# Query and key products of each half of the tokens as seven block products on shared sums, with the tokens split by quarters

## The chip, the cores and the metric

The program runs on one core of a Trainium2 chip. The core has TensorE (PE in the profile; PEld is its loading of weights), VectorE (DVE), ScalarE (ACT), GpSimd (POOL) and SyncE (SP, which here only issues DMAs). They run side by side, each in its own fixed order, and wait for one another through semaphores. The metric is the time of one execution on the device in microseconds (us), lower is better: 2119.15 us is the median of three runs before the change (2118.79 to 2119.32).

## The reference

x has 8 batches of 1024 tokens of 512 values (float32). Cut to what matters:

```python
xn = _layernorm(x)                      # LN(x)
q = xn @ Wq                             # 512 -> 128
gate = softmax(xn @ Wg)                 # 3 gates a token
for i in range(3):
    k = xn @ Wk[i]                      # 512 -> 128
    v = xn @ Wv[i]                      # 512 -> 128
    w = decay[i] ** max(s - t - 1, 0) * (s > t)
    blended += gate[..., i:i+1] * ((q @ k.T) * w) @ v
s = blended @ Wo * out_scale
h = silu(xn @ lut[gate_idx].T) * (xn @ lut[up_idx].T)     # 1376 wide
g = silu(h @ lut[down_idx].T)
out = x + s * g
```

The weights of the feed-forward are indices into a table of 16 values. q and the three k together are one product of LN(x), 512 values, with a matrix of 512 columns.

## The kernel before

The kernel has two phases. Phase 1 computes LN(x), the attention part, and the looked-up feed-forward weights, and leaves its results in DRAM. Phase 2 computes the feed-forward and the output.

**Phase 1** runs over batches b. For a batch, `project` (L361) loads x in 8 chunks of 128 tokens, last chunk first, normalises each chunk, transposes it on PE into `xnT` (pt, L411, copied by ACT at L412), and computes pv (L418), which holds v and the logits of the gates; ACT copies it out (L421). In pv the slice of `xnT` just copied is the stationary operand, which PE loads as weights. `features(hf, j)` (L448) computes for a half hf of 512 tokens q^T (j=0) or one k_i^T (j=1 to 3) as four matmuls 128x512 into one PSUM bank pq (L455), which ACT copies to `qT` or `kT` (L458). Half 1 is done while chunks 3 to 0 are projected, one j a chunk; half 0 in the first four chunk steps of the next batch.

At the same time `chunks` (L523) works on the batch before: a decayed state runs over its chunks from the last to the first. In a chunk step PE does pk (transposes of k, L552), psc (k times gated q, L561), pu (the state's update, L569), and po (L583) in two groups, first state times qb, then v times pr. Between them DVE does ga (L536, gates times q^T; the gates come from DRAM, broadcast to all partitions) and pr (L563, psc times the decays), POOL qb (L540), and ACT ks (L555), R (L588), the scaling of pu (L595) and bl (L584). The gates go through DRAM: they are written transposed (gTd, L442) and read back as ga (L446).

The step of a chunk is written out by hand: the main loop at L637 to L662 advances the generators of the older batch, the newer batch, what is left of the batch before it (`ending`), and the build of the feed-forward weights in a fixed interleaving. `keep_order` then holds the order of PE, DVE, ACT and POOL as traced; SP's order is the scheduler's. `defer` and `tick` put a DMA a few parts later. I number the steps of a batch k=0 to 7: in k=0 to 3 half 0 of the batch before gets its features, in k=4 to 7 half 1 of the batch being projected.

PSUM has 8 banks in phase 1: `p_a` with 4, shared by pt, pv and pq, `p_c` with 3, shared by pk, psc and po, and one for pu.

**Sums of LN(x)^T.** The feed-forward multiplies 2x2 blocks with seven products in place of eight, on two levels. For the outer level it needs four sums t1 to t4 of the blocks of LN(x)^T; the blocks b11, b12, b21, b22 are the two halves of the 512 values by the two halves of the tokens. DVE forms them at L512, one 128x1024 operation in each of the steps k=0 to 3, and SP writes xnT and the sums to `xs_d` (L519 to L521).

**Weights** (`ffn_weights`, L246). DVE looks up 128 rows of gate and up weights (L217 to L241), POOL forms the sums of the inner level (L270 to L274) and, for a pair of such blocks, the outer sums in `pair` (L289 to L295); the lower block's own second quarter is written by a DMA of its own (L287) and the pair's four parts by another (L296).

**Phase 2** works on PE in groups of seven products (L783, four matmuls 128x256 each), then the down projection (L1037) and the output with Wo (L1152).

Of the kernel before, what the change touches and what calls it, by code (L numbers as in the profile page):

```python
# [48 lines left out]
def recurrent_block(ctx: ExitStack, tc, x, wq, wk, wv, wo, wg, decay_logits, out_scale, lut, gidx, uidx, didx, out):  # L49
# [25 lines left out]
    U = 512  # L75
    NC = T // P
# [89 lines left out]
    def tables():  # L166

        nc.sync.dma_start(out=dl, in_=decay_logits.partition_broadcast(P))
        nc.sync.dma_start(out=lut_sb, in_=lut.partition_broadcast(P))
        nc.sync.dma_start(out=osc, in_=out_scale.partition_broadcast(P))
        nc.gpsimd.iota(e_int, pattern=[[0, NI]], base=0, channel_multiplier=1)
        nc.gpsimd.memset(e_c, float(P))
        nc.gpsimd.memset(zero, 0.0)
        nc.sync.dma_start(out=pow_d[:, :P], in_=zero)
        yield

        nc.vector.tensor_scalar(dl, dl, -87.0, None, ALU.max)  # L180
        nc.scalar.activation(dec, dl, AF.Exp, scale=-1.0)
        nc.vector.tensor_copy(e_k, e_int)
        nc.vector.tensor_tensor(lut_x, lut_i[:, :, 0:1], lut_i[:, :, 1:2], ALU.bitwise_xor)
        yield
        nc.vector.tensor_scalar(dec, dec, 1.0, None, ALU.add)
        nc.vector.reciprocal(dec, dec)
        nc.gpsimd.tensor_tensor(k_tab, dec, e_k, ALU.pow)
        nc.gpsimd.tensor_tensor(c_tab, dec, e_c, ALU.pow)

        def write():  # L190
            with nc.allow_non_contiguous_dma(reason="384 words, once"):
                nc.sync.dma_start(out=pow_d[:, P:].rearrange("i s -> s i"), in_=k_tab)

        defer(4, write)
        for _ in range(4):
            yield
        backs = []
        for step, first in ((1, 0), (0, P)):
            back = small.tile([P, NI, P], F32, name="back", tag="back", bufs=2)
            nc.sync.dma_start(  # L200
                out=back, in_=bass.AP(pow_d.tensor, pow_d.offset + first, [[step, P], [2 * P, NI], [1, P]])
            )
            backs.append(back)
        yield
        for tab, back in zip((w_tab, q_tab), backs):
            nc.vector.tensor_copy(tab, back[:, :, ::-1])
            yield
# [38 lines left out]
    def ffn_weights(build, pool, pair_pool):  # L246
# [6 lines left out]

        upper = []

        def gate_up(o):
# [28 lines left out]
            pair = pair_pool.tile([P, 7, 4, P], F32, name="pair", tag="pair")  # L285
            nc.sync.dma_start(out=to[:, :, 0:2, :], in_=up)
            defer(3, lambda: nc.sync.dma_start(out=to[:, :, 2, :], in_=low[:, :, 1, :]))  # L287
# [5 lines left out]
            nc.gpsimd.tensor_tensor(pair[:, :, 2], b11, b21, ALU.subtract)  # L293
            yield
            nc.gpsimd.tensor_tensor(pair[:, :, 3], b12, pair[:, :, 1], ALU.subtract)  # L295
            defer(4, lambda: nc.sync.dma_start(out=to[:, :, 3:7, :], in_=pair))  # L296
# [12 lines left out]
        def down(rows, e, ends):  # L309
# [21 lines left out]
            pair = pair_pool.tile([P, 7, 4, P], F32, name="pair", tag="pair")  # L331
# [10 lines left out]
            defer(4, lambda: nc.sync.dma_start(out=to[:, :, 4:7, :], in_=pair[:, :, 0:3]))  # L342
# [12 lines left out]
    def warm_up(n):  # L355

        warm = p_a.tile([P, P], F32, name="warm", tag="a")
        for _ in range(n):
            nc.tensor.matmul(warm, lhsT=ident, rhs=ident, start=True, stop=True)

    def project(b, pools, sides, kept):  # L361
# [6 lines left out]
        wvg_sb, wqk_sb = sides  # L368
# [4 lines left out]
        qT, kT = {}, {}  # L373
        gates = []
        kept[b] = (v_sb, gates, qT, kT)
# [32 lines left out]
        def transpose(c):  # L408
            pt = p_a.tile([P, NV, P], F32, name=f"pt{b}_{c}", tag="a")
            for v in range(NV):  # L410
                nc.tensor.transpose(pt[:, v, :], xts[c][:, ts(v, P)], ident)  # L411
            nc.scalar.copy(xnT[:, :, ts(c, P)], pt)  # L412

        def values(c):

            pv = p_a.tile([P, NI * D + NI], F32, name=f"pv{b}_{c}", tag="a")
# [31 lines left out]
        def features(hf, j):  # L448

            if j == 0:  # L450
                qT[hf] = att.tile([P, U], F32, name=f"qT{b}_{hf}", tag=f"qT{hf}", bufs=1)
                kT[hf] = att.tile([P, NI, U], F32, name=f"kT{b}_{hf}", tag=f"kT{hf}", bufs=1)
            pq = p_a.tile([P, U], F32, name=f"pq{b}_{hf}_{j}", tag="a")
            for v in range(NV):
                nc.tensor.matmul(  # L455
                    pq, lhsT=wqk_sb[:, v, ts(j, D)], rhs=xnT[:, v, ts(hf, U)], start=(v == 0), stop=(v == NV - 1)
                )
            nc.scalar.copy(qT[hf] if j == 0 else kT[hf][:, j - 1, :], pq)  # L458
# [23 lines left out]
        for k in range(NC):  # L482
# [11 lines left out]
            if k >= NC // 2:  # L494
                if lag and k == NC // 2:
                    values(c + 1)
                    lag = 0
                features(1, k - NC // 2)
# [4 lines left out]
            if k >= lag:  # L503
                values(c + lag)
            yield
        ts_ = tp.tile([P, 4, 2, U], F32, name=f"ts{b}", tag="ts")
        b11, b12, b21, b22 = (xnT[:, 2 * r : 2 * r + 2, ts(hf, U)] for r in (0, 1) for hf in (0, 1))
        t1, t2, t3, t4 = (ts_[:, k] for k in range(4))
        sums = ((t1, b12, b11), (t2, b22, t1), (t3, b22, b12), (t4, b21, t2))
        for k in range(NC // 2):  # L510
            yield
            nc.vector.tensor_tensor(*sums[k], ALU.subtract)  # L512
            features(0, k)
# [3 lines left out]
            next(half, None)  # L517
            yield
        nc.sync.dma_start(out=xs_d[b][:, 0:4, :], in_=xnT[:, :, :U])  # L519
        nc.sync.dma_start(out=xs_d[b][:, 4:6, :], in_=b22)  # L520
        defer(2, lambda: nc.sync.dma_start(out=xs_d[b][:, 6:14, :], in_=ts_.rearrange("p a b u -> p (a b) u")))  # L521

    def chunks(b, pools, kept):  # L523

        chk, blp = pools
        v_sb, gates, qT, kT = kept.pop(b)
# [5 lines left out]
        def gated(c):  # L532
# [3 lines left out]
            nc.vector.tensor_tensor(qa, qa, qT[hf][:, ts(k, P)].unsqueeze(1).to_broadcast([P, NI, P]), ALU.mult)  # L536
# [7 lines left out]
        for c in reversed(range(NC)):  # L544
# [3 lines left out]
            kc = kT[c // (NC // NHALF)][:, :, ts(c % (NC // NHALF), P)]  # L548
# [51 lines left out]
    def phase_1():  # L600
        nonlocal small, p_a, p_c, p_r
        with (
            tc.tile_pool(name="p_a", bufs=4, space=PSUM) as p_a,
# [17 lines left out]
            wqk_sb = wts.tile([P, NV, (NI + 1) * D], F32, name="wqk_sb", tag="wqk_sb")  # L621

# [4 lines left out]
            warm_up(12)  # L627
            kept = {}
            ending = iter(())
            newer = project(0, pools, (wvg_sb, wqk_sb), kept)  # L630
            setup = tables()
# [5 lines left out]
            for b in range(B + 1):  # L637
                following = project(b + 1, pools, (wvg_sb, wqk_sb), kept) if b + 1 < B else iter(())
                older = chunks(b - 1, (chk, blp), kept) if b else iter(())
                for k in range(NC):  # L640
# [22 lines left out]
                    if (b, k) == (0, 3):  # L663
                        keep_order(tc, seen, (mybir.EngineType.SP,))
# [14 lines left out]
    H = U // 2  # L679
    ORDER = (1, 6, 5, 7, 2, 3, 4)  # L680

    def phase_2():
        with (
# [76 lines left out]
            class Node:  # L760
# [20 lines left out]
                def product(self, n, i, start=False):  # L781
                    for a in range(2):
                        nc.tensor.matmul(  # L783
                            self.t[n][:, ts(a, H)],
                            lhsT=self.w[:, a, (0, 1, 6, 2, 3, 4, 5)[i - 1], :],
# [301 lines left out]
            def down(b, h, h_tail, bl, ahead, beside):  # L1087
# [11 lines left out]
                def load(half, pool, tag):  # L1099
                    xr[half] = pool.tile([P, 4, V], F32, name=f"gx{b}_{half}", tag=tag)  # L1100
                    for n in range(4):
                        hold(out=xr[half][:, n], in_=x[b, ts(4 * half + n, P), :])
# [47 lines left out]
                def result(k):  # L1150
                    ps = next_bank(f"ps{b}_{k}")
                    nc.tensor.matmul(ps, lhsT=bl[:, ts(k, P)], rhs=wo_sb, start=True, stop=True)  # L1152
# [4 lines left out]
                    (nc.sync if b == B - 1 else nc.gpsimd).dma_start(out=out[b, ts(k, P), :], in_=o)  # L1157
# [176 lines left out]
```

## Time and profile before

| | |
|---|---|
| median of three runs | 2119.15 us (2118.79 to 2119.32) |
| the profiled execution, its own time | 2119.36 us |
| its span | 2117.6 us |
| phase 1, from 0 to the first matmul fs (L731) of phase 2 | 603.93 us |
| phase 2 | 1513.67 us |
| one chunk step of phase 1, pk to pk, with a batch being projected (k=0 to 6) | 9.48 us |
| PE busy, 0 to 603.93 us | 601.89 us |
| DVE busy, 0 to 603.93 us | 476.51 us |
| ACT busy, 0 to 603.93 us | 359.89 us |
| POOL busy, 0 to 603.93 us | 280.43 us |
| granted clock of PE in both phases | 1.00 |

The page's lines give, for a group of instructions, the line of the program, the engine, the operation, the output and input tiles, partitions by elements, and the count; then busy time in us, the mean of one in ns, and the idle time before them with what ended it. A timeline line begins with the start in us from the span's start and the duration. A float32 matmul of the program is two PE instructions, so four matmuls are x8. The starts of successive PE lines give the time that a group takes; its printed duration includes a tail that the next group overlaps.

### The profile page before, as it was taken

The page shows a single profiled execution, that of the slowest core. Times are in us where ns is not written, and L with a number is a line of the kernel's source. Part 1 is how long each engine was busy: PE and PEld are TensorE (multiplying, and loading weights), DVE is VectorE, ACT ScalarE, POOL GpSimd, SP SyncE. Part 2 cuts the span into 40 slices and gives each one's busy share as a digit, 9 for nine tenths or more (in the row PEclk, how much of TensorE's full clock was granted, in tenths as well). Part 3 has the DMA queues.
Part 4 walks back from the last instruction along what each step waited for, and adds up shares of the span by engine and source line. Part 5 has one row for each costly group of instructions (what it writes and reads, how often), then busy time and mean ns, then how long its engine had stood idle before and what let it go on. Part 6 is the DMA issues. An engine that isn't in the chain of part 4 may idle for free.

```text
span 2117.6 us, 31134 instructions
## 1 busy us (share of the span) xinstructions
PE 2109.2 (100%) x11306; PEld 1678.6 (79%) x11306; DVE 1409.2 (67%) x2150; ACT 929.4 (44%) x2083; POOL 1021.2 (48%) x1046
## 2 busy tenths in 40 slices
PE   9999999999999999999999999999999999999999
PEld 6666666666678888887879888887978888797877
DVE  6889888678545774576567556656755665675557
ACT  3666666666434414423441442344145324423531
POOL 2554565253354537416642752655275255527432
PEclk9999999999999999999999999999999999999999
DMA  7556557565464644464455446444544634464442
GB/s 195 158 176 160 190 174 169 181 129 177 110 252 153 240 168 153 156 236 140 146 195 185 151 148 245 139 147 172 208 151 154 246 123 155 165 218 148 152 154 109
DMA packets 164271, 361.45 MB, mean 171 GB/s; under 512 B 52083, under 2 KB 90230, under 8 KB 163094
## 3 DMA queue, kind: packets, MB, share of 16 engines
q1 hardware_dynamic: 149702, 336.12, 48.7%
q0 software_dynamic: 4480, 14.68, 1.7%
q10 hardware_dynamic: 9936, 8.66, 1.4%
q8 instruction: 90, 1.47, 0.3%
q14 instruction: 63, 0.52, 0.1%
HBM read 282.87 MB, written 76.55 MB: 170 GB/s over the span
## 4 chain that ended last, share of the span: by engine, by line
PE 98%; DVE 1%; DMA 1%; POOL 0%; issue 0%; ACTq 0%; ACT 0%; SPq 0%; POOLq 0%; DVEq 0%
PE s L783 33%; PE pq L455 10%; PE pv L418 8%; PE sE L783 6%; PE s12d L1037 5%; PE s21d L1037 5%; PE s11d L1037 5%; PE po L583 4%; PE fs L731 3%; PE pd L1145 3%; PE ps L1152 3%; PE sEd L1037 2%; PE psc L561 2%; PE pu L569 2%; PE pt L411 1%; PE fsE L731 1%
## 5 line engine op out<-in xcount | busy, mean ns | idle before, releaser
L783 PE MATMUL s<-xs,wq 128*128 128x256 f32 x3264 | 731.2, 379 | 0.0
L783 PEld LDWEIGHTS s<-xs,wq 128*128 128x128 f32 x3264 | 619.6, 190 | 95.8 <-issue 8.1
L806 DVE TENSOR_TENSOR s<-s,e 128x512 f32<-128x512 f32 x136 | 95.1, 699 | 204.1 <-ACT s L805 204.0
L455 PE MATMUL pq<-xnT,wqk_sb 128*128 128x512 f32 x512 | 230.3, 592 | 0.0
L1116 POOL TENSOR_TENSOR cu<-cu 128x256 f32<-128x256 f32 x32 | 34.8, 1088 | 306.7 <-DVE cl L1115 306.7
L418 PE MATMUL pv<-wvg_sb,xnT 128*128 128x387 f32 x512 | 177.6, 489 | 0.3 <-DMA wvg_sb<-in_wv 0.3
L714 POOL TENSOR_TENSOR xs<-xs 128x256 f32<-128x256 f32 x224 | 170.8, 789 | 4.5
L455 PEld LDWEIGHTS pq<-xnT,wqk_sb 128*128 128x128 f32 x512 | 92.4, 190 | 92.1 <-issue 91.8
L810 DVE TENSOR_TENSOR sE<-s,e 128x512 f32<-128x512 f32 x136 | 95.0, 699 | 104.9 <-PE s L783 104.9
L874 POOL TENSOR_TENSOR u<-u,e 128x512 f32<-128x512 f32 x64 | 79.9, 1270 | 148.7 <-DVE u L870 130.2
L801 ACT COPY e<-sE 128x512 f32<-128x512 f32 x136 | 79.6, 585 | 138.8 <-PE sE L783 138.5
L783 PE MATMUL sE<-xs,wq 128*128 128x256 f32 x544 | 139.6, 379 | 0.0
L397 POOL TENSOR_SCALAR rstd<-rstd 128x1 f32<-128x1 f32 x56 | 27.8, 497 | 229.6 <-ACT junk L396 229.0
L418 PEld LDWEIGHTS pv<-wvg_sb,xnT 128*128 128x128 f32 x512 | 92.7, 190 | 54.8 <-issue 2.4
L878 POOL TENSOR_TENSOR h<-h,u 128x512 f32<-128x512 f32 x64 | 80.1, 1272 | 113.1 <-DVE u L885 103.5
L794 ACT COPY s<-s 128x512 f32<-128x512 f32 x136 | 77.5, 570 | 109.2 <-PE s L783 105.1
L805 ACT COPY s<-s 128x512 f32<-128x512 f32 x136 | 77.5, 570 | 97.6 <-PE s L783 97.6
L1037 PE MATMUL s12d<-wdd,z 128*128 128x128 f32 x896 | 118.5, 275 | 0.6 <-ACT s12d L1059 0.6
L783 PEld LDWEIGHTS sE<-xs,wq 128*128 128x128 f32 x544 | 103.4, 190 | 14.0
L1037 PEld LDWEIGHTS s12d<-wdd,z 128*128 128x128 f32 x896 | 109.1, 192 | 0.8 <-ACT s12d L1059 0.8
L224 DVE TENSOR_SCALAR leaf<-idx,lut_x,lut_sb 128x1024 int32<-128x1024 int32 (+2 forms) x119 | 101.3, 876 | 0.0
L563 DVE TENSOR_TENSOR pr<-psc,w_tab 128x384 f32<-128x384 f32 x64 | 35.5, 555 | 92.0 <-PE psc L561 91.8
(236 smaller groups left out, 4254.3 us busy)
## 6 DMA issues: line engine op xcount, KB each, us to landing
wq<-quadd SPq DMA_DIRECT2D x112, 896.0 KB, 4.5
wdd<-wdd SPq DMA_DIRECT2D x56, 896.0 KB, 4.8
xs<-xsd SPq DMA_DIRECT2D x56, 512.0 KB, 6.6
wq<-quadd SPq DMA_DIRECT2D x48, 448.0 KB, 4.1
x<-in_x SPq DMA_DIRECT2D x64, 256.0 KB, 5.9
xsd<-ts SPq DMA_DIRECT2D x8, 2048.0 KB, 7.5
gx<-in_x SPq DMA_DIRECT2D x64, 256.0 KB, 5.4
out<-gx POOLq DMA_DIRECT2D x56, 256.0 KB, 2.3
```

What stands on the lines that cost most here:

```text
L224: nc.vector.tensor_scalar(o.bitcast(I32), iv, lut_x[:rows, k, :], lut_i[:rows, k, 0:1], ALU.bitwise_and, ALU.bitwise_xor,)
L418: nc.tensor.matmul(pv, lhsT=xnT[:, v, ts(c, P)], rhs=wvg_sb[:, v, :], start=(v == 0), stop=(v == NV - 1))
L455: nc.tensor.matmul(pq, lhsT=wqk_sb[:, v, ts(j, D)], rhs=xnT[:, v, ts(hf, U)], start=(v == 0), stop=(v == NV - 1))
L583: nc.tensor.matmul(po, lhsT=lh, rhs=rh, start=(n == 0), stop=(n == len(prods) - 1))
L714: nc.gpsimd.tensor_tensor(o, x1, x2, ALU.subtract)
L731: nc.tensor.matmul(ps, lhsT=w[:, 2 * W_OF[k] + n, :m], rhs=xs[:, X_OF[k], 2 * n : 2 * n + 2, :], start=start and n == 0, stop=stop and n == 1,
L783: nc.tensor.matmul(self.t[n][:, ts(a, H)], lhsT=self.w[:, a, (0, 1, 6, 2, 3, 4, 5)[i - 1], :], rhs=self.xs[:, X_OF[self.ks[a]], D_OF[i], : ...
L806: nc.vector.tensor_tensor(self.t[1], self.t[1], self.e, ALU.add)
L810: nc.vector.tensor_tensor(self.t[3], self.t[2], self.e, ALU.add)
L874: nc.gpsimd.tensor_tensor(o[:, n], o[:, n], other[:, n], ALU.add)
L878: nc.gpsimd.tensor_tensor(of_h(half, n), of_h(half, n), two(other[:, n]), ALU.mult)
L1037: nc.tensor.matmul(self.t[n][:, ts(a, P)], lhsT=self.lhs[i][:, e, ts(a, P)], rhs=self.w[:, e, D_OF[i], :], start=start and a == 0 and e == ...
```

## The change

q^T and the three k_i^T of a half are now one 2x2 block product of seven products. The blocks of the weights are [512 values in two halves] by [q and k_0, k_1 and k_2]; the blocks of LN(x)^T are the two halves of the 512 values by two quarters of 256 tokens. POOL forms the four sums of the weights once (`sums_of_weights`), after step k=3 of batch 0. DVE forms the sums t1 to t4 of LN(x)^T for each half, in steps k=4 and 5 (half 1) and k=0 and 1 (half 0); the same sums go to DRAM for the feed-forward, so its outer split of the tokens is now even and odd quarters instead of halves, and the last part of phase 2 takes its rows of x, bl and the output in that order (`place`).

A product is four matmuls 128x256. The seven lie in four steps, in this order: 1 and 5, 6 and 2, 7 and 3, then 4. In k=0 to 3 the second of a step stands on PE between psc and pv; in k=4 to 7 it stands behind pv. Partial results run on in PSUM: ACT copies bank pa to pb and pb to pc, later products add to them, and there are 6 ACT copies and 2 DVE additions a half in place of 4 ACT copies.

The four banks of `p_a` are now pa, pb, pe and pc; pt and pv move to the three banks of `p_c`. `write_banks` gives two of the banks their first write from PE, by 8 of the 12 matmuls with which PE was warmed up. The `pair` tile of the weights has three parts instead of four, one sum is formed in the place of b21, and two DMAs become one; for the block rows from 8 on POOL's third sum comes four parts later.

```diff
-        def features(hf, j):
...
-            pq = p_a.tile([P, U], F32, name=f"pq{b}_{hf}_{j}", tag="a")
-            for v in range(NV):
-                nc.tensor.matmul(
-                    pq, lhsT=wqk_sb[:, v, ts(j, D)], rhs=xnT[:, v, ts(hf, U)], start=(v == 0), stop=(v == NV - 1)
-                )
-            nc.scalar.copy(qT[hf] if j == 0 else kT[hf][:, j - 1, :], pq)
+        def features(hf):
+            qk[hf] = att.tile([P, NI + 1, U], F32, name=f"qk{b}_{hf}", tag=f"qk{hf}", bufs=1)
+            c11, c12, c21, c22 = (qk[hf][:, 2 * j : 2 * j + 2, ts(c, H)] for j in (0, 1) for c in (0, 1))
+            ts_ = tp.tile([P, 4, 2, H], F32, name=f"ts{b}_{hf}", tag=f"ts{hf}")
+            b11, b12, b21, b22 = (xnT[:, 2 * v : 2 * v + 2, ts(2 * hf + c, H)] for v in (0, 1) for c in (0, 1))
+            t1, t2, t3, t4 = (ts_[:, k] for k in range(4))
+            a11, a12, s3, a22 = (wqk_sb[:, 2 * v : 2 * v + 2, ts(j, 2 * D)] for j in (0, 1) for v in (0, 1))
+            s1, s2, s4 = (wqs[:, k] for k in range(3))
+            lhs = {1: a11, 2: a12, 3: s4, 4: a22, 5: s1, 6: s2, 7: s3}
+            rhs = {1: b11, 2: b21, 3: b22, 4: t4, 5: t1, 6: t2, 7: t3}
+            pa, pb, pe, pc = (p_a.tile([P, 2, H], F32, name=f"{r}{b}_{hf}", tag=r) for r in ("pa", "pb", "pe", "pc"))
+            def product(ps, k, start=False):
+                for j in range(2):
+                    for v in range(2):
+                        nc.tensor.matmul(
+                            ps[:, j, :],
+                            lhsT=lhs[k][:, v, ts(j, D)],
+                            rhs=rhs[k][:, v, :],
...
+            there = xs_d[b][:, :, ts(hf, H)]
+            nc.vector.tensor_tensor(t1, b12, b11, ALU.subtract)
+            yield
+            product(pa, 1, True)
+            nc.scalar.copy(pb, pa)
+            nc.vector.tensor_tensor(t2, b22, t1, ALU.subtract)
+            nc.sync.dma_start(out=there[:, 0:4, :], in_=xnT[:, :, ts(2 * hf, H)])
+            yield
+            product(pe, 5, True)
+            nc.scalar.copy(c21, pe)
+            nc.vector.tensor_tensor(t3, b22, b12, ALU.subtract)
+            nc.sync.dma_start(out=there[:, 4:6, :], in_=b22)
+            yield
+            product(pb, 6)
+            nc.scalar.copy(pc, pb)
+            nc.scalar.copy(c12, pb)
+            nc.vector.tensor_tensor(t4, b21, t2, ALU.subtract)
+            defer(2, lambda: nc.sync.dma_start(out=there[:, 6:14, :], in_=ts_.rearrange("p a b u -> p (a b) u")))
+            yield
+            product(pa, 2)
+            nc.scalar.copy(c11, pa)
+            yield
+            product(pc, 7)
+            nc.vector.tensor_tensor(c22, pc, c21, ALU.add)
+            yield
+            product(pe, 3)
+            nc.vector.tensor_tensor(c12, pe, c12, ALU.add)
+            yield
+            product(pc, 4)
+            nc.scalar.copy(c21, pc)
+            yield
...
-            pt = p_a.tile([P, NV, P], F32, name=f"pt{b}_{c}", tag="a")
+            pt = p_c.tile([P, NV, P], F32, name=f"pt{b}_{c}", tag="c")
...
-            pv = p_a.tile([P, NI * D + NI], F32, name=f"pv{b}_{c}", tag="a")
+            pv = p_c.tile([P, NI * D + NI], F32, name=f"pv{b}_{c}", tag="c")
...
+    def sums_of_weights(wqk_sb, wqs):
+        a11, a12, a21, a22 = (wqk_sb[:, 2 * v : 2 * v + 2, ts(j, 2 * D)] for j in (0, 1) for v in (0, 1))
+        s1, s2, s4 = (wqs[:, k] for k in range(3))
+        nc.gpsimd.tensor_tensor(s1, a21, a22, ALU.add)
+        nc.gpsimd.tensor_tensor(s2, s1, a11, ALU.subtract)
+        nc.gpsimd.tensor_tensor(a21, a11, a21, ALU.subtract)
+        nc.gpsimd.tensor_tensor(s4, a12, s2, ALU.subtract)
...
-            tc.tile_pool(name="p_a", bufs=4, space=PSUM) as p_a,
+            tc.tile_pool(name="p_a", bufs=1, space=PSUM) as p_a,
...
+            if o >= 4 * NQ:
+                for _ in range(4):
+                    yield
+            nc.gpsimd.tensor_tensor(b21, b11, b21, ALU.subtract)
+            defer(3, lambda: nc.sync.dma_start(out=to[:, :, 2:4, :], in_=low))
...
+                def place(k):
+                    odd, quarter, a = k // 4, k // 2 % 2, k % 2
+                    return 4 * quarter + 2 * odd + a
```

## The prediction

> **What bounds the kernel now.** I read the page's busy shares and chain first, then who waited for whom on PE (TensorE), then single chunks of phase 1 in the timeline.
>
> ```profile
> PE 2109.2 (100%) x11306; PEld 1678.6 (79%) x11306; DVE 1409.2 (67%) x2150; ACT 929.4 (44%) x2083; POOL 1021.2 (48%) x1046
> PE 98%; DVE 1%; DMA 1%; POOL 0%; issue 0%; ACTq 0%; ACT 0%; SPq 0%; POOLq 0%; DVEq 0%
> L783 PE MATMUL s<-xs,wq 128*128 128x256 f32 x3264 | 731.2, 379 | 0.0
> L455 PE MATMUL pq<-xnT,wqk_sb 128*128 128x512 f32 x512 | 230.3, 592 | 0.0
> ```
>
> PE runs without a break, and the chain of waits is PE over 98%. In the list of PE's waits the longest after the start is "PE s12d L1037 <- ACT" with 0.6 us, once; nothing in the chunks of phase 1 (0 to 603.9 us) makes PE wait. So each us taken from PE is gained, and each new wait of PE is lost, one for one. The second thing to see is how full the others are: in 0 to 603.93 us the windows give DVE 476.5, ACT 359.9, POOL 280.4 us. DVE is no reserve: of the 9.48 us of a chunk it is busy 9.3 to 9.4 in about twenty chunks.
>
> One chunk, PE with ACT, batch 1 being projected:
>
> ```profile
> 158.02 0.49 PE L552 MATMUL pk<-ident,kT 128*128 128x128 f32 x3
> 158.22 0.27 ACT L584 COPY bl<-po 128x128 f32<-128x128 f32 x1 [1.53 <-PE po L583]
> 158.35 0.60 PE L411 MATMUL pt<-ident,x 128*128 128x128 f32 x4
> 158.78 3.60 PE L455 MATMUL pq<-xnT,wqk_sb 128*128 128x512 f32 x8
> 160.66 0.60 ACT L412 COPY xnT<-pt 128x512 f32<-128x512 f32 x1
> 162.22 0.83 PE L561 MATMUL psc<-ga,kT 128*128 128x128 f32 x6
> 162.89 2.77 PE L418 MATMUL pv<-wvg_sb,xnT 128*128 128x387 f32 x8
> 165.50 0.83 PE L569 MATMUL pu<-v,ks 128*128 128x128 f32 x6
> 167.51 0.49 PE L552 MATMUL pk<-ident,kT 128*128 128x128 f32 x3
> ```
>
> Read starts, not durations: pk 0.33, pt 0.43, pq 3.44, psc 0.67, pv 2.61, pu and the two halves of po 2.01. pv's weights are the xnT slice that ACT (ScalarE) copies in the same chunk: the copy ends at 161.26, and pq lies between it and pv.
>
> **1. Products on PE.** Removed: 4 groups pq for each half of a batch, at 3.44 us. Added: 7 products of 4 matmuls 128x256, 8 instructions each. That form exists in phase 2:
>
> ```profile
> 629.52 5.34 PE L783 MATMUL s<-xs,wq 128*128 128x256 f32 x24
> 634.70 1.03 PE L783 MATMUL sE<-xs,wq 128*128 128x256 f32 x4
> 635.57 5.34 PE L783 MATMUL s<-xs,wq 128*128 128x256 f32 x24
> ```
>
> From 629.52 to 635.57 lie 28 instructions: 0.216 us each, a product is 1.73. A half falls from 13.76 to 12.09 us, by 1.67; 16 halves: **-26.7**. The 12 matmuls at the start are the same number before and after.
>
> The Trainium skill speaks against it: "TensorE: Matmul & The Clock Gate", section "Back-to-back issue gap", has a sustained spacing of 81 ns at 128 columns and 131 at 512, so halving the columns should not halve the time; with some 98 ns at 256 (my estimate between its two) a half would cost 18.0 us and the change would lose 68 us. The rows here differ, 0.216 against 0.430, exactly half, and the measurement decides.
>
> **2. pv waits for ACT.** In the chunks of half 1 (k=4 to 6) and in the last of half 0 (k=3) only one product of 1.73 lies before psc instead of 3.44; the other comes behind pv, or is not there. PE would load pv's weights at 162.78-1.71=161.07, but xnT is there only at 161.26 plus about 0.05, the gap from "pr" to the weight load at 571.5. ACT does not finish earlier: its run bl, R, pu, ks, xnT begins when po ends (at 158.22, after 1.53 idle) and lasts 3.04. So 0.24 a chunk. The older batch must be there (batches 1 to 7): 28 chunks, **+6.7**. Bounds: 0.13 if only matmul start counts, 0.33 with a whole weight load (0.19) in the open: 3.6 to 9.2. Behind pv on PE stands everything else of the chunk.
>
> **3. First chunk of batch 1.**
>
> ```profile
> 42.24 0.33 SPq L446 DMA_DIRECT2D ga<-gTd  x1
> 47.62 0.56 DVE L536 TENSOR_TENSOR ga<-ga,qT 128x384 f32<-128x384 f32 x1 [6.69 <-DMA ga<-gTd]
> 48.09 1.30 DVE L241 COPY_PREDICATED wgu<-bit,leaf 128x1024 f32<-128x1024 uint8 x1
> 50.73 0.83 PE L561 MATMUL psc<-ga,kT 128*128 128x128 f32 x6
> ```
>
> DVE (VectorE) waits here for the gates from DRAM. PE will want psc 1.67+1.72 earlier, at 47.3; ga is ready at 48.2: 0.9. The fifth product then stands next on PE and needs t1, behind ga and a copy on DVE: 48.2+1.2+0.7=50.0, while psc ends at 48.9: another 1.1. **+2.0**; bounds 0 (gates 2 us sooner) and 3.4 (all that PE was ahead).
>
> **4. DVE.** Removed: 4 sums of 128x1024 a batch, 1.21 each, all in half 0. Added: 8 sums of 128x512 at 0.68 (L1005 z<-h, phase 2) and 4 adds out of PSUM at 0.70 (L806): half 0 loses 0.7 us a batch, half 1 gains 4.1. The path is pr, which the second half of po waits for:
>
> ```profile
> 97.49 0.72 PE L561 MATMUL psc<-ga,kT 128*128 128x128 f32 x5
> 101.23 0.56 DVE L563 TENSOR_TENSOR pr<-psc,w_tab 128x384 f32<-128x384 f32 x1
> 102.11 0.83 PE L583 MATMUL po<-pr,v 128*128 128x128 f32 x6
> ...
> 231.12 0.55 DVE L563 TENSOR_TENSOR pr<-psc,w_tab 128x384 f32<-128x384 f32 x1
> 231.73 0.94 PE L583 MATMUL po<-pr,v 128*128 128x128 f32 x6
> ```
>
> pr was done 0.32 and 0.05 us before PE needed it. The change helps and hurts: psc comes 1.72 earlier in the chunk, and where a product follows it PE reaches po no sooner, but at k=3 and k=7 1.72 sooner. I carried DVE's lateness through the 56 chunks: each pr at its old arrival plus the added sums so far, not before psc, and PE held to pr's end. With 0.68 a sum only batches 1 and 2 touch PE, 0.5 us in all after the wait of step 3; with 0.85 (sums stretched as 1.21 was to a mean of 1.45) 3.0; with 1.1 (stretched as the 2.02 seen at 226.80) 8.9. I take **+2.0**, bounds 0.5 and 8.9. The last chunk's step at 231 keeps clear because DVE's 0.7 saved lies just ahead of it.
>
> **5. ACT, POOL, SP.** ACT: 6 copies of 0.57 a half for 4; three of them in k=1 and k=5 eat 1.14 of the 1.53 idle before bl, so they are hidden as long as ACT is on time. It is not when POOL's rstd is late (ACT waited 2.8 us for it in all, once 2.1): then bl, and with it xnT and pv of the next chunk, slip. **+1.0**, bounds 0 and 3. POOL: four sums of weights 128x512, 1.27 each by L874, at about 18 to 23 us, where POOL sat idle 6.83 before 27.5 and the fifth product comes at 25.4: 0; without that cover 5 us late for the sixth product. In the FFN weights as many operations run as before, in place, so 0. SP: three more DMAs a batch, 0.4 to 1.2 us to issue; it stands waiting for gTd 153 us in all, and x is loaded some three chunks ahead: 0. PSUM: pt and pv move to the three banks of pk, psc and po, five tiles a chunk. pt needs the bank of the pv before (copied 1.66 before pt), psc that of po, pk that of psc; all free in time by the rows above, 0; a late ACT is in the 0 to 3. Phase 2 does the same instructions on other rows of x and out: 0.
>
> **Sum** against the profiled execution, 2119.36 us (span 2117.6, 1.8 around it; 0.2 above the median): -26.7+6.7+2.0+2.0+1.0 = -15.0: **2104.4**. With all bounds good -22.6, 2096.8; with all bad -2.2, 2117.2.
>
> **Rivals.**
> *Everything stays covered* (15 in 100): xnT is out in time because ACT's run starts a little sooner, the gates land sooner: only 1 to 4 us of waits, -24.5, 2095. For it: 0.13 is a small gap. Against: ACT's run of 3.04 was the same in every chunk I looked at.
> *DVE becomes the bound* (20): the 4.1 us more in half 1 fall on full chunks and the sums run at 1.1: step 4 at 8.9, -8, 2111. For it: margins of 0.05 to 0.5 in five chunks, and POOL stretches DVE's rows (1.0 to 2.0 for 1.21). Against: from batch 5 on DVE idles 3 to 8 us in half 1.
> *ACT falls behind PE* (10), the slower case: with 6 copies a half, ACT reaches bl after po has ended, and the run to xnT holds pv in every chunk of batches 1 to 7, not in 28. It decides from about 0.5 us late on average: 56 times (0.5+0.1) is 33.6, so -26.7+33.6 = +7, 2126. For it: bl, R, pu, ks, xnT is one in-order run that the next pv needs. Against: 6.3 us busy in 9.48, 1.5 idle before bl and 1.46 before v.
> *It gives back what it saves* (5): waits of several kinds take 24 to 29 us, 2119.
> *The forecast* has 50: 2100 to 2109.
>
> **Range and chances.** 2096 to 2117 takes in the forecast and DVE's case and most of the covered one. 0.2% is 4.2 us, what a measurement of this kernel tells from none. Faster: 50+15+18 of DVE's = 0.83; same 5+2 = 0.07; slower 0.10.
>
> **What will show it.** The products start 1.73 us apart where two follow each other; the chain shows PE waiting for xnT (its copy, on ACT) some 0.24 us in 28 chunks; psc at about 48 us with a wait for ga and then one for ts; waits for pr only before about 200 us; phase 2 begins some 15 us earlier and is as long as before. I am wrong if PE waits for a PSUM bank (for v, bl, or the copies pb and pc), if waits for pr go on beyond batch 3, or if phase 2's length changes.

## The result and the profile after

The changed kernel took 2125.16 us (median of 13 runs, 2119.97 to 2129.02), the kernel before, beside it, 2119.12 (2118.79 to 2120.59): ratio 1.0027, 95% interval 1.0019 to 1.0036. It is slower by 0.27%, where 2104.4 was predicted. The runs also spread over 9 us, where those of the kernel before spread over 1.8. The profiled execution took 2122.76 us, span 2121.0; its mean granted clock of PE was 0.997, and 1.000 before.

From the page of the changed kernel: the busy times, the chain of waits, and the group of pv's weight loads (busy, mean ns, idle before it and what ended most of that).

```profile
PE 2096.5 (99%) x11690; PEld 1756.2 (83%) x11690; DVE 1436.3 (68%) x2214; ACT 946.1 (45%) x2115; POOL 1028.3 (48%) x1050
...
PE 82%; DVE 2%; POOL 0%; issue 0%; ACT 0%; DMA 0%; POOLq 0%; ACTq 0%; DVEq 0%
...
L434 PEld LDWEIGHTS pv<-wvg_sb,xnT 128*128 128x128 f32 x512 | 94.2, 190 | 58.5 <-ACT xnT L428 4.7
```

PE is busy 12.7 us less and the span is 3.4 us longer. The shares of the chain add up to 84% only, and so they do in a kernel below that is 10 us faster, so its 82% for PE is no measure of the loss. The list of PE's waits is (line, what it waited for: us in total, times, longest):

```profile
PE po L658 <- DVE pr L638: 5.1, 5, 1.6
PE fs L809 <- ACT t L819: 4.7, 1, 4.7
PE psc L636 <- DVE ga L611: 2.7, 1, 2.7
PE pt L427 <- ACT v L437: 1.8, 1, 1.8
PE pe L484 <- DVE ts L494: 1.6, 3, 0.8
...
PE fs L809 <- DMA wq<-quadd: 1.0, 1, 1.0
```

One line of this list lies behind phase 1, in which the prediction expected nothing: fs waits 4.7 us for ACT. The timeline there (all engines; start, duration, and in brackets the idle time before):

```profile
600.70 3.65 PE L809 MATMUL fs<-xs,wr 128*96 128x512 f32 x8 [0.97 <-DMA wq<-quadd]
602.16 1.30 DVE L242 COPY_PREDICATED wgu<-bit,leaf 128x1024 f32<-128x1024 uint8 x1
...
604.18 1.88 PE L809 MATMUL fsE<-xs,wr 128*96 128x512 f32 x4
...
606.45 0.32 SPq L328 DMA_DIRECT2D wdld<-wgu  x1
...
610.10 0.58 ACT L819 COPY t<-fs 96x512 f32<-96x512 f32 x1 [10.06 <-DMA wdld<-wgu]
...
610.73 3.73 PE L809 MATMUL fs<-xs,wr 128*96 128x512 f32 x4 [4.67 <-ACT t L819]
```

ACT's first copy of phase 2 waits for a DMA of phase 1: the last looked-up block wgu is copied on DVE until 603.46, summed on POOL, and written to DRAM from 606.45 on; only when that has landed does ACT write t. Before the change the same copy began 2.0 us after the first fs, 0.9 us after that write had been issued, and waited for PE alone:

```profile
603.93 3.67 PE L731 MATMUL fs<-xs,wr 128*96 128x512 f32 x8 [0.35 <-ACT bl L584]
...
605.10 0.32 SPq L323 DMA_DIRECT2D wdld<-wgu  x1
...
605.97 0.58 ACT L741 COPY t<-fs 96x512 f32<-96x512 f32 x1 [2.09 <-PE fs L731]
```

Windows of the same kernel (length, busy us of PE, PEld, DVE, ACT and POOL with instructions, then the granted clock, the DMA share and GB/s):

```profile
46.00:49.00 3.00, 1.32 (x7) 0.81 (x5) 0.00 (x0) 2.94 (x8) 0.25 (x1) 1.00 0.78 275
49.00:52.00 3.00, 1.09 (x7) 0.93 (x8) 2.56 (x4) 0.95 (x3) 2.36 (x3) 0.99 1.08 391
52.00:55.00 3.00, 3.00 (x8) 2.37 (x9) 2.97 (x5) 0.21 (x1) 2.92 (x4) 0.50 1.07 393
...
606.00:612.00 6.00, 1.33 (x3) 0.68 (x3) 0.69 (x1) 1.15 (x3) 5.84 (x9) 0.69 0.37 153
```

After PE has stood, the clock is granted at half: from 51.9 to 55.3 us (3.41 us), and from 608.3 to 615.1 (6.83). PE is "busy" there, but at half speed; a list of waits doesn't hold this loss. It costs 1.7 and up to 3.4 us.

Where the 18.4 us between the predicted 2104.4 and the profiled 2122.76 are. Steps are measured from pk to pk; the last row is the time from the first fs on and the wait just ahead of it:

| place | before -> predicted | measured |
|---|---|---|
| half 1 of batch 0, up to the first pk | -1.67 | -1.88 |
| first step of batch 1 (8.81 us before) | +2.0 | +5.80 |
| a batch with no other wait (6 and 7) | -2.38 | -2.34, -2.33 |
| waits of DVE and ACT in batches 1 to 5 | +3.0 | +10.4 |
| first fs to the end, and its wait for loads | 0 | +7.2 |

The three rows that are off give 3.8 + 7.4 + 7.2 = 18.4. The first step of a batch took 8.81 us before the change, not the 9.48 of the steps behind it. The measured column is one execution; in the profiles of e1, e2, e4 and e9 below, whose edits leave the gates' way untouched, ga came 2.8 to 3.8 us after the first pk, against 4.75 here, and the same step took 11.72 to 13.64 us instead of 14.61.

### The profile page after: what moved, and what is told of

It is laid out like the page before. It is cut to its first block, busy times and chain, and to the rows that moved or that the text cites. A ratio compares the mean times of both kernels' runs of the same rounds, so it can differ in the third digit from the quotient of the medians.

```text
span 2121.0 us, 32151 instructions
## 1 busy us (share of the span) xinstructions
PE 2096.5 (99%) x11690; PEld 1756.2 (83%) x11690; DVE 1436.3 (68%) x2214; ACT 946.1 (45%) x2115; POOL 1028.3 (48%) x1050
## 4 chain that ended last, share of the span: by engine, by line
PE 82%; DVE 2%; POOL 0%; issue 0%; ACT 0%; DMA 0%; POOLq 0%; ACTq 0%; DVEq 0%
PE s L861 33%; PE sE L861 6%; PE s12d L1115 5%; PE s21d L1115 5%; PE s11d L1115 5%; PE fs L809 3%; PE pv L434 3%; PE pd L1228 3%; PE ps L1235 3%; PE sEd L1115 2%; PE po L658 2%; PE fsE L809 1%; PE s11d L1126 1%; PE s21d L1126 1%; PE s12d L1126 1%; PE sEd L1126 1%
## 5 line engine op out<-in xcount | busy, mean ns | idle before, releaser
L615 POOL TENSOR_TENSOR qb<-ga,q_tab 128x384 f32<-128x384 f32 x56 | 69.0, 1232 | 62.7 <-DVE ga L611 51.6
L242 DVE COPY_PREDICATED leaf<-bit,leaf 128x1024 f32<-128x1024 uint8 (+2 forms) x68 | 90.5, 1330 | 1.5
L1239 POOL TENSOR_TENSOR gx<-gx,cu 128x512 f32<-128x512 f32 x32 | 40.8, 1280 | 82.0 <-DVE cu L1237 64.5
```

Source lines behind the costliest of these rows:

```text
L242: nc.vector.copy_predicated(o, bits[level - 1][:rows, :n], t[:rows, :n])
```

## The experiments

All were run beside the kernel before, whose median lay between 2119.0 and 2119.3 us each time; the changed kernel, with its 2125.16, was not run again beside them. The theory to begin with: three losses that the prediction did not have (a placement in SBUF at the start of phase 2, PE's clock, and DVE's waits for the wgu buffers), beside the one wait that it had right (xnT).

**e1: wqs above the wgu buffers.** In the changed kernel the pools lie one above the other, and wqs (6144 bytes a partition) lies below the wgu buffers. By the program's memory map the buffers end at byte 144960 of a partition instead of 138816, and phase 2's t begins at 143872.

```diff
+            tc.tile_pool(name="wqp", bufs=1) as wqp,
             tc.tile_pool(name="att", bufs=2) as att,
...
-            wqs = wts.tile([P, 3, 2, 2 * D], F32, name="wqs", tag="wqs")
+            wqs = wqp.tile([P, 3, 2, 2 * D], F32, name="wqs", tag="wqs")
```

> The changed kernel with the sums of the weights (wqs, 6 KB a partition) placed above the two wgu buffers instead of below them, nothing else. Theory (placement): in the changed kernel wqs moves the wgu buffers up by 6144 bytes, so that they reach 1088 bytes into the room of phase 2's first t, and the ACT copy of fs to t waits for the last looked-up block, its sums on POOL and its write to DRAM; PE then stands 4.67 us and runs 6.83 us at half clock. Without the overlap the wait and these two clock windows go: 8.1 us less than the changed kernel, phase 2 as long as before the change (1514 us from the first fs), profile near 2114, median 2115 to 2118. Rival (late lookups): the last lookups end late on DVE and POOL whatever the placement, and the first t or the sums of xs wait for them all the same: at most 2 us less, the half clock at the start of phase 2 stays.

2112.39 us (2111.56 to 2112.96), ratio to before 0.9967 (0.9955 to 0.9978). The timeline at the same place:

```profile
597.71 3.65 PE L810 MATMUL fs<-xs,wr 128*96 128x512 f32 x8 [0.56 <-DMA wq<-quadd]
...
599.59 1.31 DVE L242 COPY_PREDICATED wgu<-bit,leaf 128x1024 f32<-128x1024 uint8 x1
599.72 0.58 ACT L820 COPY t<-fs 96x512 f32<-96x512 f32 x1 [2.27 <-PE fs L810]
...
602.91 3.60 PE L810 MATMUL fs<-xs,wr 128*96 128x512 f32 x8
...
603.88 0.32 SPq L328 DMA_DIRECT2D wdld<-wgu  x1
```

ACT now waits only for PE, and writes t 4 us before wgu is even sent off. No stretch has half clock, and from the first fs to the end it takes 1513.2 us (1520.3 in the changed kernel, 1513.7 before). The gain, 12.8 us, is more than the 8.1 expected: here the first step of batch 1 took 11.93 instead of 14.61 us, since ga came 1.2 us sooner and the clock did not fall there either, and the medians hold clock losses that a single profile need not show.

**e2: PE kept busy in the first chunk.** 11 and 3 matmuls of the identity fill the two places where PE stood.

```diff
             product(pa, 1, True)
+            if (b, hf) == (0, 0):
+                idle_work(pe, 11)
...
+            if (b, hf) == (0, 0):
+                idle_work(pe, 3)
             product(pe, 5, True)
```

> The changed kernel with 14 matmuls 128x128 of the identity more, 11 of them on PE ahead of the first chunk's psc and 3 ahead of its fifth product, into a bank that the fifth product then starts anew; their results are not used. Theory (clock follows PE's idleness): the half clock from 51.9 to 55.4 us comes from PE having stood 2.75 and 0.84 us just before; with PE busy there the granted clock stays 1.00 and the first step of batch 1 is 1.7 us shorter (12.9 instead of 14.6), the median about 1.7 us lower. Rival (the clock falls for another cause, such as the burst of DMAs or a fixed time): the half clock stays at about 52 us, and the step is as long as before or longer by what the matmuls stretch it.

2121.49 us (2119.59 to 2124.16), 3.7 less than the changed kernel. The first step of batch 1 took 11.96 us instead of 14.61, with 14 matmuls more in it. Windows of this kernel:

```profile
49.00:52.00 3.00, 3.00 (x28) 2.97 (x28) 2.93 (x6) 1.91 (x6) 1.59 (x3) 1.00 1.08 388
52.00:55.00 3.00, 3.00 (x13) 2.22 (x12) 3.00 (x5) 0.59 (x1) 2.92 (x5) 1.00 1.08 379
```

The DMA traffic is the same (388 and 379 GB/s for 391 and 393), and the clock stays at 1.00: the burst of DMAs alone does not halve it. Not all of the shorter step is the clock's: ga also came 2.0 us sooner after the first pk than in the changed kernel's profile. And in the profiles of e1 and e4, without the added matmuls, the clock stayed at 1.00 here too, with waits of 1.75 and 1.54 us for ga in place of 2.75; so this run alone does not settle what halves the clock, and the count of windows at the end has to support it. The half clock at the start of phase 2, which this kernel leaves alone, is still there.

**e3: the lower block sent off earlier.** The sum in place of b21 comes second, and its DMA one part later.

```diff
-            defer(3, lambda: nc.sync.dma_start(out=to[:, :, 2:4, :], in_=low))
+            defer(1, lambda: nc.sync.dma_start(out=to[:, :, 2:4, :], in_=low))
```

> The changed kernel with POOL's sums of a pair in another order: the sum formed in place of b21 directly after the first sum, and the lower block's DMA one part later instead of three; the other two sums follow. Theory (buffers): DVE's 12.2 us of waits for a wgu buffer (POOL pair 7.0, DMA quadd 5.2; 2.0 before the change) are what makes pr late; the wait for the DMA falls from 5.2 to under 1.5, pr waits of PE at 235 and 301 us go (2 to 3 of 5.1 us), time 2 to 3 us less. Rival (DVE's added sums make pr late, as the prediction had it): DVE idles less but pr is as late, PE's waits for pr stay at 4 to 6 us, time within 1 us.

2120.57 us (2118.61 to 2123.67). The time came out lower, the mechanism did not: DVE's wait for the DMA fell only from 5.2 to 4.6 us, that for POOL rose from 7.0 to 9.3, and PE waited 5.7 us for pr. Two steps became shorter by 0.9, one longer by 0.4. That points to POOL's whole chain of eight sums as what holds the buffers, rather than the DMA behind it.

**e4: ACT's scaling of pu behind the copy of xnT.**

```diff
-                for i in range(NI if c > 1 and not at_end else 0):
-                    nc.scalar.mul(pu[:, i, :], pu[:, i, :], c_tab[:, i : i + 1])
+                if c > 1 and not at_end:
+                    behind_xnT.append(scale)
...
             nc.scalar.copy(xnT[:, :, ts(c, P)], pt)
+            while behind_xnT:
+                behind_xnT.pop()()
```

> The changed kernel with ACT's scaling of pu (1.09 us) moved behind the copy of xnT in each chunk step. Theory (ACT's run is what pv waits for): xnT is out 1.09 us earlier, the 0.26 us that the steps k=3 to 6 are longer go, 28 times: 6.5 to 7 us less; step k=3 falls from 8.02 to about 7.8 and k=4 and 5 from 9.75 to 9.49. Rival (the 0.26 is the loading of pv's weights or the bank of pv, not ACT): the steps keep their length, time within 1 us. Other rival: the scaling now makes pu late, and PE waits before pu: time not less.

2119.53 us (2117.39 to 2122.11), 5.6 less. The steps show it better than the time, since in this profile the first step of batch 1 is 2.9 us shorter as well, with no half clock in it. Step k=3 took 7.78 us (8.02), k=4 and 5 took 9.50 (9.75), and no weight load of pv waits for xnT any more: step 2 of the prediction is confirmed. Some of it went back: PE waited 3.5 us for t1 instead of 1.6, and 2.5 for pt's bank instead of 1.8.

**e5: three edits together.** e1 and e4, and t1 of half 0 at the end of step k=7, with the fifth product of batch 0 ahead of the first psc.

```diff
+            if k == NC - 1:
+                of_half = features(0)
+                next(of_half)
             yield
-        of_half = features(0)
```

> Three edits on the changed kernel: wqs placed above the wgu buffers (as in e1), the scaling of pu behind the copy of xnT (as in e4), and the first sum t1 of half 0 formed on DVE at the end of step k=7 instead of behind ga in k=0, with the fifth product of batch 0 ahead of the first psc. Theory (each wait is its own and they add): against e1's 2112.4 the 28 waits for xnT go (-6.9, of which e4 gave back some 2), the wait for t1 (1.4 to 3.5 us over the batches) goes, and the first chunk's wait for ga shrinks from 1.8 to about 0: 2102 to 2105. Rival (what is taken from one wait is given to the next: pr, the copy of v, the end of the lookups): 2109 or more.

2111.07 us (2110.16 to 2113.5): the rival. The first step fell to 10.39 us and the wait for xnT went, but PE's waits for pr rose from 5.2 in e1 to 8.5 us and DVE's for a wgu buffer from 15.0 to 20.7, and the clock was halved twice, at 231 and 354 us.

**e6: the next block begun two parts later.** e1, and this:

```diff
             defer(4, lambda: nc.sync.dma_start(out=to[:, :, 4:7, :], in_=pair))
-            for _ in range(3):
+            for _ in range(5):
                 yield
```

> e1's kernel with the next block's lookups begun two parts later after each pair of gate and up blocks. Theory (buffers): pr is late because DVE, in order, stands for up to 5 us before it may write the next block into a wgu buffer that POOL's sums and the DMA of the pair still hold; two parts later the buffer is free, DVE's waits on it fall from 12 to under 4 us and PE's waits for pr from 5.2 to under 2; the last lookups end later (10 parts): 1 to 3 us less than e1, 2110 to 2111.5. Rival (the added sums t1 to t4 fill DVE): the waits on wgu fall but those for pr stay at 4 to 6 us, time as e1 or above.

2126.92 us (2123.8 to 2128.88), missed, though the theory's part shows: the waits for pr at 107, 170, 235 and 301 us are gone, but in the step at 229 one for qb of 2.6 us came instead, and that step took 12.18 us for e1's 9.88. DVE's waits for a wgu buffer fell from 15.0 to 7.0 us, not under 4, and PE's waits for pr are 3.9 in all, 3.5 of it at 585.6, where the lookups ran late. The pk of batch 7 began at 484.32 instead of 489.85. But the lookups then ended at 611.7 us. DVE's first add of phase 2 stood behind them, PE waited 7.1 us and ran 6.83 us at half clock.

**e8: t3 and t4 on POOL.** e1, with two of the four sums moved off DVE.

```diff
-            nc.vector.tensor_tensor(t3, b22, b12, ALU.subtract)
+            nc.gpsimd.tensor_tensor(t3, b22, b12, ALU.subtract)
```

> e1's kernel with t3 and t4 formed by POOL instead of DVE. Theory (buffers): DVE is relieved of 2.7 us a batch, but POOL's chain of sums, which holds the wgu buffers and rstd, gets some 5 us a batch longer: the waits for pr stay (4 to 7 us) and ACT waits longer for rstd; time as e1 or up to 4 us more. Rival (the prediction's step 4, DVE filled by the added sums): with half of the added sums gone from DVE the waits for pr fall from 5.2 to under 2.5 us, and the time by 2 to 3 us to about 2110.

2130.43 us (2128.66 to 2131.74). With half of the added sums gone from DVE, PE waited 11.4 us for pr (5.2 in e1) and the clock fell four times. So less work on DVE did not bring pr sooner. It does not clear the sums of blame, since the edit also lengthened POOL's chain: DVE's waits for a wgu buffer rose from 15.0 to 20.2 us. In the step where e1's PE waited 1.23 us at 104.1, t3 and t4 had stood between the wait for the buffer and pr; without them PE still waited 0.88 us there.

**e9: the changed kernel without the four parts of delay.** wgu still overlaps t.

```diff
-            if o >= 4 * NQ:
-                for _ in range(4):
-                    yield
             nc.gpsimd.tensor_tensor(b21, b11, b21, ALU.subtract)
```

> The changed kernel without the four parts by which it delays POOL's third sum for the block rows from 8 on; wqs stays where the change put it. Theory (the wait at the start of phase 2 needs two things, the placement and lookups that end late): the last copies of the lookups end some 4.5 to 5 us earlier (about 599 instead of 603.5), the write of the last block lands by about 605.5, before PE needs the first t, and the wait of 4.67 us and the half clock of 6.83 us go although wgu still overlaps t: 7 to 9 us less than the changed kernel, median 2115 to 2118. Rival (placement alone): the wait at the start of phase 2 stays above 3 us, median 2122 or more.

2116.84 us (2115.13 to 2119.43), ratio 0.9987 (0.9978 to 0.9997). The last copy of the lookups began at 598.92 instead of 602.16 us. ACT still waited for the write of wgu, but PE only 1.1 us, and the clock did not fall there. So the loss at the start of phase 2 is a product of two parts of the change: the place of wqs, and lookups that end later while PE arrives sooner. Either one alone costs about 1 us or nothing: from the first fs to the end it is 1514.6 us here and 1513.2 in e1, for 1513.7 before the change.

**e7, e10, e11: the lookups brought forward.** e7 is e5 with e6's edit, a part more in every other step of batches 5 to 7, and phase 2's wr loaded ahead of xs. e10 is e6 with those parts alone. e11 is e7 without the four parts of delay, with the larger number from batch 4 on and two parts fewer in the first step of batch 1.

```diff
-                    build_some(busy * (2 + (b > 0 and k % 2 == 0)))
+                    build_some(busy * (2 + (b > 0 and (k % 2 == 0 or b > 4))))
...
             xs = room_for_x(0)
+            first_w = weights_of(0, NO - 1)
```

> e5's three edits, e6's two parts, four parts of the lookups more in each of batches 5 to 7, and the weights of phase 2's first products loaded ahead of the seven loads of xs. Theory (waits add, and DVE has room after batch 5): e5 less 2 to 4 us, 2098 to 2102, the waits for pr under 2 us, no wait at phase 2's start. Rival: the lookups crowded into batches 5 to 7 make pr late there, or the first sums of xs wait for the lookups' end, and it is no better than e5.

> e6's kernel (wqs above wgu, the next block begun two parts later) with the lookups made up for by four parts more in each of batches 5 to 7. Theory (buffers make pr late; e6 lost it all again because the lookups ended 10 parts later): the gains that e6 had up to batch 6 (its steps were 5.5 us ahead of e1's there) stay, no wait at the start of phase 2: 2107 to 2109.5 against e1's 2112.4. Rival (DVE and POOL have no room, the work only moves): pr and the copy of v wait in batches 5 to 7 instead, 2111.5 or more.

> e7's kernel without the four parts of delay for the block rows from 8 on, with the larger number of parts from batch 4 on, and with two parts fewer in the first step of batch 1. Theory (the waits left in e7 are the lookups': pr at 54.8 with 1.98, and the end at 552 to 578 with 1.6): both go, 2102 to 2105. Rival (the parts taken from one step make another late): 2106 to 2108.

e7: 2106.31 us (2106.07 to 2107.97); no wait and full clock at the start of phase 2, but PE still waited 5.7 us for pr, 2.7 for pt's bank and 2.2 for qb. e11: 2106.96 (2105.85 to 2107.53), no better; in its profile qb came 3.2 us late at 166.0 and the clock fell behind it.

e10: 2118.69 (2115.55 to 2121.54), missed again at the start of phase 2. At batch 7 it was 4.4 us ahead of e1. Then, in windows of e10:

```profile
594.00:597.00 3.00, 3.00 (x26) 2.69 (x24) 3.00 (x5) 0.27 (x1) 0.00 (x0) 1.00 1.03 393
597.00:600.00 3.00, 0.05 (x1) 0.00 (x0) 1.57 (x2) 0.27 (x1) 1.24 (x2) 0.88 1.14 360
600.00:603.00 3.00, 2.45 (x3) 0.97 (x4) 0.00 (x0) 0.00 (x0) 2.92 (x5) 0.50 0.98 366
```

PE stands for 3.5 us ahead of the first fs, with the DMAs at 360 to 393 GB/s. Seven loads of xs of 512 KB were issued from 585.92 us on and wr behind them. The profile names no releaser, so that wr was late is read from the traffic and not shown by itself; e7, e11 and e12, which load wr first, have no wait there.

**e12: POOL's four sums apart.** e11 with two parts between POOL's sums of a pair.

```diff
             nc.gpsimd.tensor_tensor(pair[:, :, 0], b21, b22, ALU.add)
             yield
+            yield
             nc.gpsimd.tensor_tensor(pair[:, :, 1], pair[:, :, 0], b11, ALU.subtract)
             yield
+            yield
```

> e11's kernel with two parts instead of one between POOL's four sums of a pair, the lower block's DMA one part after its sum, four parts behind the pair instead of five, and the larger number of parts from batch 3 on. Theory (POOL's four sums of 2.1 to 2.6 us in a row hold qb and rstd, which hold po and ACT's x, ks and v): e7's waits for qb (2.2 at 226.8) and for the copy of v (2.7 at 482.5) go, against e11 2 to 4 us less: 2099 to 2103. Rival (POOL's work is the same, the buffers are held longer): pr waits grow by as much, no better than e11.

2103.32 us (2101.62 to 2105.68, 4 runs), ratio to before 0.9926 (0.9911 to 0.9940): the fastest of all. PE's waits in it:

```profile
PE po L668 <- DVE pr L648: 3.0, 4, 2.0
PE pt L428 <- ACT v L440: 2.1, 1, 2.1
...
PE psc L646 <- ACT junk L412: 1.0, 1, 1.0
```

Phase 2 begins at 586.49 us, and DVE waits for a wgu buffer 1.5 us in all. Of the waits for pr, 2.0 us are in the first step of batch 1. e12 holds many edits at once, so its time is not the worth of any one of them.

## Why the prediction was wrong

PE's own work and the wait for xnT came as forecast. What failed is the rule behind step 4 (waits for pr, +2.0), two terms put at 0 in step 5, the size of step 3, and the premise that a wait of PE costs no more than its own length.

**Products on PE: right.** -26.7 by 0.216 us an instruction. A chunk of the changed kernel, PE alone:

```profile
528.26 0.49 PE L627 MATMUL pk<-ident,qk 128*128 128x128 f32 x3
528.59 0.60 PE L427 MATMUL pt<-ident,x 128*128 128x128 f32 x4
529.03 1.89 PE L484 MATMUL pa<-xnT,wqk_sb 128*128 128x256 f32 x8
530.76 0.83 PE L636 MATMUL psc<-ga,qk 128*128 128x128 f32 x6
531.56 2.88 PE L434 MATMUL pv<-wvg_sb,xnT 128*128 128x387 f32 x8
534.28 1.89 PE L484 MATMUL pe<-ts,wqs 128*128 128x256 f32 x8
536.00 0.83 PE L644 MATMUL pu<-v,ks 128*128 128x128 f32 x6
```

The products take 1.73 and 1.72 us from start to start.

**pv waits for ACT: right.** psc at 530.76 to pv at 531.56 is 0.80 us for psc's 0.67, and pv takes 2.72 for 2.61: 0.24 together. The page has 4.7 us of weight loads waiting for xnT, and that in 28 places, the number predicted; in the steps it is 0.25 to 0.28 each, 7.3 us for the 6.7 predicted. e4 takes it away.

**First chunk of batch 1: right mechanism, sized 2.0, measured 5.8.** Two terms were missing. I held ga at the old kernel's time; it was ready to use at 49.41 us instead of 47.62, for its read was issued at 43.15 (42.24 before), behind a write issued at 31.33 (28.96), and took 6.3 us until ga could be used (5.4); no run shows what lengthened it. And 1.7 us are PE at half clock, of which the prediction has nothing.

**DVE and pr: the step that failed in phase 1.** "I carried DVE's lateness through the 56 chunks: each pr at its old arrival plus the added sums so far" supposes that DVE's other waits stay. They did not. DVE's waits in the first 604 us, changed kernel:

```profile
DVE qk L516 <- PE pc L484: 28.4, 9, 8.6
...
DVE pr L638 <- PE psc L636: 9.1, 10, 1.9
...
DVE wgu L225 <- POOL pair L300: 7.0, 2, 5.0
...
DVE wgu L225 <- DMA quadd<-wgu: 5.2, 2, 5.0
```

and in the kernel before:

```profile
DVE pr L563 <- PE psc L561: 91.8, 35, 7.9
...
DVE wgu L224 <- POOL pair L295: 2.0, 1, 2.0
```

Before, DVE stood 91.8 us for psc. Now psc comes earlier in the step; 28.4 us of waiting stand ahead of one of the new adds, which needs pc, and elsewhere DVE runs on to the next block and stands there up to 5 us, with ga and pr behind it. The rows of DVE at three of PE's waits for pr (at 107.04, 235.38 and 301.12 us):

```profile
99.22 0.81 DVE L225 TENSOR_SCALAR wgu<-idx,lut_x,lut_sb 128x1024 int32<-128x1024 int32 x1 [4.99 <-POOL pair L300]
...
106.43 0.56 DVE L638 TENSOR_TENSOR pr<-psc,w_tab 128x384 f32<-128x384 f32 x1
...
222.60 2.42 DVE L611 TENSOR_TENSOR ga<-ga,qk 128x384 f32<-128x384 f32 x1
...
230.82 0.81 DVE L225 TENSOR_SCALAR wgu<-idx,lut_x,lut_sb 128x1024 int32<-128x1024 int32 x1 [0.18 <-DMA quadd<-wgu]
...
234.78 0.55 DVE L638 TENSOR_TENSOR pr<-psc,w_tab 128x384 f32<-128x384 f32 x1
...
296.68 0.81 DVE L225 TENSOR_SCALAR wgu<-idx,lut_x,lut_sb 128x1024 int32<-128x1024 int32 x1 [4.98 <-DMA quadd<-wgu]
```

At 107 and 301, and with 1.99 us at 170, pr lies behind a wait for a wgu buffer. At 235, the longest of PE's waits for pr, it does not: DVE waited 0.18 us there and was otherwise busy from 219.5 us on, behind a wait of 5.68 for pc and with stretched rows (2.42 us for a ga that takes 0.55 as a rule). At 107 and 170 two of the added sums lie between the buffer and pr as well, 2.2 and 2.1 us, more than the 1.21 and 0.51 that PE waited. So the buffers are a cause that the prediction left out, but not shown to be the only one: e6, with the same sums and a later block, has none of the four waits, and e12 has 1.5 us of buffer waits and 3.0 of waits for pr, but both edits also move the work of the lookups, and e8 fits either reading. How the loss divides between buffers, sums and stretched rows stays open. The sums themselves took 0.81 us on average, between the 0.68 and 0.85 for which the prediction had 0.5 and 3.0 us; the steps in which PE waited for pr are 6.4 us longer than the same steps of batches 6 and 7 (sized +2.0, bounds 0.5 to 8.9). Another 1.5 us are waits for t1 in the first steps of batches 2 to 4, which the prediction had for batch 1 alone. ACT's wait for rstd, sized +1.0, was right in kind: ACT stood 5.05 us for it once, and PE 1.75 for the bank that ACT then copied late, the one wait for a PSUM bank that the prediction named as a sign of being wrong.

**"In the FFN weights as many operations run as before, in place, so 0" and "Phase 2 does the same instructions on other rows of x and out: 0": wrong, 7.2 us together.** The operations were as many, but four parts later, and phase 2 had the same instructions on other addresses: the prediction never asked where wqs lies in SBUF. e1 takes all of it away, e9 all but 1 us. The prediction's own sign, "phase 2's length changes", is what came.

**PE's clock: left out.** Of the 13 runs, that with a mean clock of 0.999 took 2119.97 us, the seven with 0.997 took 2122.8 to 2125.2, the four with 0.996 took 2126.0 to 2129.0 (one with 0.998: 2125.6). Waits of 2 to 5 us, priced one for one, cost up to 1.7 us more for each 3.41 us of half clock.

The slower rival gave 2126, near the time, but by ACT holding pv in all chunks, which did not happen: that nearness is luck. With most waits removed by other edits e12 comes out at 2103.3, so the saving on PE was there to be had, and the change as made gave it back. That this is near 2104.4 does not confirm the sum: e12 also takes away the wait for xnT, which the sum had at +6.7.

## What to carry to other kernels

An added tile moves every pool above it: look up which later tile then lies on which earlier buffer, and when that buffer is released, before a phase is called unchanged. Where an in-order engine loses one wait, follow it to the next thing that it will wait for, and who stands behind it there; if the work on that chain is the same, the wait has only moved. Where PE is the bound, price a wait of about 2 us or more with the clock that it can cost as well: waits of 1.83 (e8) and 2.24 us (e5) were followed by half clock, one of 1.98 (e7) was not.

## What the hardware showed

PE's clock fell each time by half, for 3.41 or 6.83 us, and the falls of one execution lie whole numbers of 3.41 us apart (163.0 between the two of the changed kernel, 51.93 and 608.30 us). Some came after much less than 3.41 us of standing still. In the changed kernel the two gaps ahead of the first fall were 2.75 and 0.84 us, with 0.9 us of work between, and 2.4 us of them lie in the last 3.41 us before the fall. Counting PE's busy share in windows of 3.41 us laid against the falls, from 25 us on to 8 us before the end, in the profiles of the changed kernel and all twelve experiments: all windows with a share of 0.40 or less were followed by half clock, none with 0.485 or more (away from a stretch that was already at half), and between them both occurred (0.42 in e7 without a fall, 0.48 in e9 with one). Traffic does not decide it: the windows before the falls have from 0 GB/s (e5, at 354 us) to 390 (e9, at 52). Once at half, a window with 0.79 was not enough to lift it (e4: 6.83 us); one with 1.00 was (the changed kernel, at 52 us).

The Trainium skill, "TensorE: Matmul & The Clock Gate", section "What's actually happening", has the window of 3413 ns, free-running, and the half rate, as seen here. Its section "HAM oscillation — how this bites in real kernels" gives the rule "no PE-idle gaps >~3.4µs"; the runs here differ, since a single gap of 2.24 us (e5, at 351.2) and one of 1.83 (e8, at 599.3) were enough.
